# Expert jobs of a routed feed-forward block: the list one slot earlier, one-hots spread over the slots, the row eviction on ScalarE, three slots for most bits of the second search

## The chip, the cores and the metric

The kernel runs on one core of a Trainium2 chip. The metric is the device time of one execution in microseconds, the median of several runs. TensorE (PE, with its weight loads shown as PEld) multiplies matrices and transposes through an identity; VectorE (DVE) and ScalarE (ACT) read its results from PSUM; GpSimd (POOL) issues the indirect transfers that gather and scatter rows by index; SyncE (SP) issues the plain transfers. Each engine takes its own instructions in the order of the program[...].

## The reference

An attention block is followed by a routed feed-forward block. Sixteen sequences of 256 tokens, width 256, pass through layer norms, attention with 16 heads and an output projection, and leave 4096 token rows. What matters here is the second half:

```
tok = x.reshape(-1, d)
gate = jax.nn.softmax(tok @ Wgate.T, axis=-1)
k_cap = bs // E                                   # 4096 // 8 = 512
vals, idx = jax.lax.top_k(gate.T, k_cap)          # each expert takes its 512 best tokens
w = vals.T
g = _ln(tok[idx_flat], mlp_g, mlp_b).reshape(k_cap, E, d)
y = gelu(einsum('ked,ehd->keh', g, fc1s) + b1s)   # 256 -> 1024
y = einsum('keh,edh->ked', y, fc2s) + b2s         # 1024 -> 256
tok = tok.at[idx_flat].add((y * w[..., None]).reshape(-1, d))
```

Each of 8 experts chooses its 512 tokens with the largest gate, normalises those rows, runs a two-layer network on them, scales the result by the gate and adds it back to the token rows.

## The kernel before

The first 930 us are the attention of the 16 sequences, laid out by a table of due times (`plan`). The table also holds the first routing and expert job 0 and most of the list of job 1. After it stands a loop written out by hand, the part that the change touches.

**Two routings.** The 512 tokens of an expert are found in two halves of 256. The first routing (`first`) looks at sequences 0 to 14 only (30 tiles of 128 tokens), so it can be done while the last sequence is still at work. The second (`second`) looks at all 32 tiles, without the tokens already chosen. So there are 16 jobs of 256 rows: jobs 0 to 7 from the first routing, jobs 8 to 15 from the second.

**The search.** A routing finds each expert's threshold bit by bit, 30 bits from 29 to 0. One bit is a round trip: `compare` (L776, DVE) counts the gates that reach the candidate, `count` (L783, PE) adds the counts over the partitions with a tiny bf16 matmul, and `drop` and `step` (L788, L795, DVE) make the next candidate. After the last bit come `masks`, `totals`, `place`, `turn_places` and `split` (L806 to L849), which give every chosen token its place among the 256. `second_routing` is a generator that hands out one list of such steps per slot; it is empty in many slots.

**A job.** `load` (L869 to L873, SP) fetches the weights w1 and w2, 1 MB each, and the bias b2. `gives` (L879, L887, DVE) prepares the values that the list carries, `onehot` (L897, DVE) one 128x128 bf16 one-hot matrix per token tile, `list_matmul` (L906, PE) multiplies the two over 30 or 32 tiles into the list of 256 token numbers and gates, `take` (L914 to L920, DVE) turns it into indices, and `gather` (L925, POOL) fetches the 256 rows in two indirect transfers of 128. `transposes` (L934, PE) turns the rows into `px`, `evict` (L941) scales and shifts them into `xT`. `up` and `gelu` (L953 on PE, L960 on ACT) are the first layer, `down` (L969, PE) the second, `finish` (L975, L976, DVE) adds the bias and multiplies by the gate, `scatter` (L979, POOL) adds the rows to the output, twice per job.

**The slots.** Job k (k = 1 to 15) runs in 16 slots. Slots 0 to 7 each hold one `up` and its `gelu`; slots 8 to 15 each a quarter of a `down`, with `finish` and `scatter` at the ends of slots 11 and 15. Everything else is placed in these slots by hand: the steps of the second routing first, then work for job k+1 (`new`: its remaining one-hots, its list, its transposes) and for job k+2 (`far`: its `gives` and first one-hots). The order of the calls in a slot is the order on each engine, so a DVE step waits behind every DVE step called before it. At the end of job k stands `far.load()`: w1 of job k+2 needs the buffer of w1 of job k and so goes out when the eight `up` are done, w2 after the last `down`. In job 7 (`late`), the next job is the first of the second routing, whose places are only known by then, so all its one-hots are made in job 7 itself.

Of the kernel before, what the change touches and what calls it, by code (L numbers as in the profile page):

```python
# [12 lines left out]
AF = mybir.ActivationFunctionType  # L13
ALU = mybir.AluOpType
# [11 lines left out]
NT = NTOK // P  # L26
# [3 lines left out]
FC = DD // P  # L30
# [7 lines left out]
LN1_G, LN1_B, B_ADA, MLP_G, MLP_B = 0, 2, 4, 6, 8  # L38
# [5 lines left out]
def kernel(  # L44
# [14 lines left out]
    nc = tc.nc  # L59
# [7 lines left out]
    vec = const.tile([P, NVEC], F32, name="vec")  # L67
# [306 lines left out]
    if True:  # L374
# [80 lines left out]
        class First:  # L455
# [22 lines left out]
            def evict(self):  # L478
                b = self.b
                hTs[b] = seq.tile([P, DC, N], F32, tag="hT", name=f"hT{b}")  # L480
                for c in range(DC):
                    nc.scalar.activation(
                        hTs[b][:, c, :], self.pt[:, c, :], AF.Identity,
                        bias=bias1[:, c, b : b + 1],
                        scale=vec[:, LN1_G + c : LN1_G + c + 1],
                    )
# [258 lines left out]
        class Routing:  # L745
# [46 lines left out]
            def step(self, n):  # L792

                old, self.cand = self.cand, bit.tile([P, 1], I32, tag="cand", name="cand")
                nc.vector.scalar_tensor_tensor(  # L795
                    self.cand, self.dropped, (1 << n) >> 1, old,
                    ALU.bitwise_or, ALU.bitwise_xor,
                )
# [62 lines left out]
        class Job:  # L861
# [76 lines left out]
            def evict(self):  # L938
                self.xT = seq.tile([P, DC, CAPL], F32, tag="hT", name="xT")
                for c in range(DC):  # L940
                    nc.vector.tensor_scalar(  # L941
                        self.xT[:, c, :], self.px[:, c, :],
                        vec[:, MLP_G + c : MLP_G + c + 1], vec[:, MLP_B + c : MLP_B + c + 1],
                        ALU.mult, ALU.add,
                    )
                self.hid = seq.tile([P, FC, CAPL], F32, tag="qT", name="hid")
                self.y = work.tile([P, KL, D], F32, tag="pr", bufs=6, name="y")
                self.ph, self.py = {}, {}
# [57 lines left out]
        for b in range(B):  # L1006
# [3 lines left out]
            a = First(b)  # L1010
# [4 lines left out]
            for (g, t), p in its["group"].items():  # L1015
                a = Group(b, g, t)
# [6 lines left out]
            for (d, *ij), p in its["quad"].items():  # L1023
                a = quads[d]
# [6 lines left out]
            for t in range(TB):  # L1031
                a = Tail(b, t)
# [17 lines left out]
        jobs = [Job(e, r, n) for r, n in ((first, n1), (second, NT)) for e in range(E)]  # L1050
# [17 lines left out]

        def second_routing():
            a, b = stretches[2], second
            yield from ([a.shift], [a.exp], [a.divide, a.parts], [], [b.turn], [b.evict])
            new = [partial(b.compare, 29)]
            for n in range(29, -1, -1):
                yield new
                yield []
                new = [partial(f, n) for f in (b.count, b.drop, b.step)]
                new.append(partial(b.compare, n - 1) if n else b.masks)
            yield from (new, [], [b.totals, b.place], [], [], [], [b.turn_places], [b.split])  # L1080

        rest = second_routing()
        last = len(jobs) // 2 - 2
        jobs[2].load()
        jobs[2].gives()
        jobs[2].onehot(0, NT // 2)
        for k in range(1, len(jobs)):
            a = jobs[k]
            new = jobs[k + 1] if k + 1 < len(jobs) else None
            far = jobs[k + 2] if k + 2 < len(jobs) else None  # L1090
            late = k == last + 1
            for s in range(2 * FC):
                for step in next(rest, ()):
                    step()
                if new and s < 4:
                    if late and s == 0:
                        new.gives()
                    h = 0 if late else NT // 2
                    w = (NT - h) // 4
                    new.onehot(h + w * s, h + w * s + w)  # L1100
                if new and s == (7 if late else 6):
                    new.list_matmul(0, NT)
                    new.take()
                    new.gather()
                if new and s == 14:
                    new.transposes()
                    new.evict()
                if far and k != last and s in (9, 10, 12, 13, 15):
                    if s == 9:
                        far.gives()  # L1110
                    else:
                        w = {10: 0, 12: 1, 13: 2, 15: 3}[s]
                        far.onehot(w * NT // 8, (w + 1) * NT // 8)
                if s < FC:
                    a.up(s)
                    a.gelu(s)
                else:
                    i, q = divmod(s - FC, 4)
                    a.down(i, 2 * q, 2 * q + 2)
                    if q == 3:  # L1120
                        a.finish(i)
                        a.scatter(i)
            if far:
                far.load()
# [50 lines left out]
```

## Time and profile before

| | before |
|---|---|
| median of 3 runs | 1227.76 us (1226.0 to 1229.04) |
| the profiled execution | 1229.52 us, its span 1227.8 us |
| PE busy | 1175.4 us (96%) |
| DVE busy | 777.0 us (63%) |
| ACT busy | 602.2 us (49%) |
| POOL busy | 590.7 us (48%) |
| mean granted TensorE clock | 0.989 |

Length of jobs 1 to 14, from the start of the first `up` of one job to that of the next (the timeline of PE gives the starts; the table of windows gives the lengths and the DVE busy time):

| job | 1 | 2 | 3 | 4 | 5 | 6 | 7 | 8 | 9 | 10 | 11 | 12 | 13 | 14 |
|---|---|---|---|---|---|---|---|---|---|---|---|---|---|---|
| us | 20.91 | 17.21 | 17.22 | 17.20 | 17.35 | 16.03 | 17.64 | 16.14 | 15.92 | 16.27 | 16.31 | 15.87 | 16.11 | 15.14 |
| DVE busy | 15.30 | 14.25 | 14.25 | 14.23 | 15.40 | 5.39 | 12.31 | 9.03 | 9.02 | 9.03 | 9.02 | 9.02 | 9.03 | 5.68 |

All times are of one execution and count from the start of its span. A line of the timeline gives the start, the length, the engine, the source line and the operation with its output and inputs, a count of merged instructions, and in brackets how long the engine had been idle and what ended that. A float32 matmul shows as two records, so "x8" of a 128x256 matmul is four matmuls, two slots. In the table of windows each engine's busy time in a stretch stands with its number of instructions, and "PEclk" is the share of the TensorE clock that was granted. Lengths of PE records overlap, since matmuls are pipelined; starts are used for sums.

### The profile page before, as it was taken

The numbers are of one execution on the slowest core, as the hardware profiler recorded it, in microseconds if no ns is written. First come the engines' busy times: TensorE is split into PE (matmuls) and PEld (weight loads), VectorE is DVE, ScalarE is ACT, GpSimd is POOL, SyncE is SP. The second block draws the span as 40 slices with busy tenths as digits, with TensorE's granted clock in tenths as the row PEclk, the third lists the DMA queues.
The fourth block names the chain that finished last, engine by engine and source line by source line (L and its number), as shares of the span: only waits on it lengthen the run. The fifth ranks groups of instructions, "written<-read, shape, count | busy, mean of one in ns | idle before, by whom it ended". The sixth has DMA issues, their size and how long they took to land. (4 is left out here: it accounts for less than half of the span.)

```text
span 1227.8 us, 19464 instructions
## 1 busy us (share of the span) xinstructions
PE 1175.4 (96%) x6784; PEld 812.7 (66%) x6784; DVE 777.0 (63%) x2276; ACT 602.2 (49%) x1669; POOL 590.7 (48%) x818
## 2 busy tenths in 40 slices
PE   6999999999999999999999999999977899999996
PEld 3556666667576666666675766667645777888885
DVE  7556665756665666657566656665677488565551
ACT  2655565555555555655555555557562312222221
POOL 4555555645455555556454555555654223323332
PEclk9999999999999999999999999999988999999998
DMA  5000000000000000000000000000200565555561
GB/s 181 1 1 5 22 6 22 9 18 14 14 15 13 27 5 23 5 22 10 18 15 13 18 10 26 6 14 14 95 1 14 177 179 148 170 174 161 162 178 26
DMA packets 46739, 62.41 MB, mean 51 GB/s; under 512 B 3888, under 2 KB 39984, under 8 KB 46640
## 3 DMA queue, kind: packets, MB, share of 16 engines
q1 hardware_dynamic: 39808, 52.70, 12.9%
q0 software_dynamic: 6144, 8.39, 3.9%
q8 instruction: 54, 0.88, 0.3%
q14 instruction: 45, 0.37, 0.1%
q10 hardware_dynamic: 688, 0.06, 0.0%
HBM read 48.56 MB, written 12.58 MB: 50 GB/s over the span
## 5 line engine op out<-in xcount | busy, mean ns | idle before, releaser
L608 POOL TENSOR_SCALAR pr<-pr,sums 128x256 f32<-128x256 f32 x512 | 238.7, 484 | 276.8 <-DVE sums L604 258.5
L506 PE MATMUL pm<-wq,hT 128*128 128x512 f32 x768 | 357.4, 604 | 5.4 <-DMA wq<-in_wqkvT 3.4
L597 ACT ACTIVATE pr<-sc,nmax 128x256 f32<-128x256 f32 x512 | 236.4, 476 | 162.5 <-DVE nmax L588 148.0
L82 POOL TENSOR_TENSOR ss<-ss,neghalf 128x8 f32<-128x8 f32 x128 | 210.4, 1648 | 99.0 <-DVE ss L527 96.7
L506 PEld LDWEIGHTS pm<-wq,hT 128*128 128x128 f32 x768 | 138.1, 192 | 148.9 <-issue 138.7
L588 DVE TENSOR_REDUCE nmax<-sc 128x2 f32<-128x512 f32 x256 | 164.5, 681 | 45.6 <-PE sc L581 45.5
L960 ACT ACTIVATE hid<-ph,vec 128x256 f32<-128x256 f32 x128 | 60.2, 473 | 209.0 <-PE ph L953 206.2
L523 DVE TENSOR_REDUCE ss<-sq 128x8 f32<-128x512 f32 x128 | 87.4, 683 | 108.8 <-ACT sq L519 108.7
L617 PEld LDWEIGHTS pp<-ident,pr 128*128 128x128 f32 x1024 | 118.5, 143 | 34.9 <-issue 19.6
L617 PE MATMUL pp<-ident,pr 128*128 128x128 f32 x1024 | 137.8, 275 | 3.3 <-ACT pr L597 2.5
L635 PE MATMUL po<-prT,v 128*64 128x256 f32 x1024 | 137.7, 391 | 0.7 <-ACT oT L645 0.7
L581 PE MATMUL sc<-kT,qT 64*128 64x256 f32 x1024 | 131.2, 394 | 0.0
L519 ACT ACTIVATE sq<-pm 128x512 f32<-128x512 f32 x128 | 77.1, 602 | 91.5 <-PE pm L506 90.2
L953 PE MATMUL ph<-xT,w 128*128 128x256 f32 x512 | 121.0, 388 | 0.6 <-DVE xT L941 0.5
L659 PE MATMUL pw<-wo,oT 128*128 128x256 f32 x512 | 119.3, 386 | 0.0
L581 PEld LDWEIGHTS sc<-kT,qT 64*128 64x128 f32 x1024 | 94.7, 188 | 34.8 <-issue 23.6
L969 PE MATMUL py<-w,hid 128*128 128x256 f32 x512 | 117.0, 381 | 0.0
L953 PEld LDWEIGHTS ph<-xT,w 128*128 128x128 f32 x512 | 95.7, 192 | 17.8 <-issue 3.5
L979 POOL DMA_INDIRECT out<-y,idx x32 | 51.1, 1596 | 116.6 <-DVE y L976 35.9
L597 ACT ACTIVATION_READ_ACCUMULATOR pr<-sc,nmax 128x1 f32 x512 | 105.8, 207 | 0.0
L659 PEld LDWEIGHTS pw<-wo,oT 128*128 128x128 f32 x512 | 96.2, 193 | 13.1 <-issue 0.8
L625 DVE COPY prT<-pp 128x512 f32<-128x512 f32 x112 | 76.9, 687 | 43.6 <-PE pp L617 42.7
(118 smaller groups left out, 1295.7 us busy)
## 6 DMA issues: line engine op xcount, KB each, us to landing
w<-in_fc1T SPq DMA_DIRECT2D x16, 1024.0 KB, 5.4
w<-in_fc2T SPq DMA_DIRECT2D x16, 1024.0 KB, 5.4
xs<-in_x SPq DMA_DIRECT2D x16, 256.0 KB, 2.8
out<-tok SPq DMA_DIRECT2D x32, 128.0 KB, 1.7
xn_dram<-tn SPq DMA_DIRECT2D x32, 128.0 KB, 1.7
wq<-in_wqkvT SPq DMA_DIRECT2D x6, 512.0 KB, 8.7
b<-in_b2s SPq DMA_DIRECT2D x16, 128.0 KB, 5.4
wo<-in_woutT SPq DMA_DIRECT2D x1, 1024.0 KB, 10.2
```

The source lines that it names most:

```text
L82: nc.gpsimd.tensor_tensor(dst, src, neghalf[:, : src.shape[1]], ALU.pow)
L506: nc.tensor.matmul(self.pm, hTs[self.b][:, c, bass.ts(self.t, P)], wq[:, c, bass.ts(self.g, GW)], start=(c == 0), stop=(c == DC - 1),)
L523: nc.vector.tensor_reduce(self.ss[:, 0, :], self.sq.rearrange("p (h d) -> p h d", d=HD), AX.X, ALU.add,)
L581: nc.tensor.matmul(self.sc[i, j][:, t, :], qTs[self.b][rows, hp, bass.ts(t, P)], kTs[self.b][rows, hp, :], start=True, stop=True,)
L588: nc.vector.tensor_reduce(self.nmax[i, j], self.sc[i, j], AX.X, ALU.max, negate=True)
L597: nc.scalar.activation(self.pr[i, j][:, t, :], self.sc[i, j][:, t, :], AF.Exp, bias=self.nmax[i, j][:, t : t + 1], scale=1.0, accum_out=se ...
L608: nc.gpsimd.tensor_scalar(self.pr[i, j][:, t, :], self.pr[i, j][:, t, :], self.sums[i][:, 1, j, t : t + 1], 1.0, ALU.mult, ALU.mult,)
L617: nc.tensor.transpose(self.pp[i, j][:, c, bass.ts(t, P)], self.pr[i, j][:, t, bass.ts(c, P)], ident,)
L635: nc.tensor.matmul(self.po[j * HD : (j + 1) * HD, i, :], vs[self.b][:, c, bass.ts(4 * self.d + 2 * i + j, HD)], self.prT[i, j][:, c, :], s ...
L659: nc.tensor.matmul(self.pw, oTs[self.b][:, hp, bass.ts(self.t, P)], wo[:, hp, :], start=(hp == 0), stop=(hp == HP - 1),)
L953: nc.tensor.matmul(self.ph[f], self.w1[:, c, bass.ts(f, P)], self.xT[:, c, :], start=(c == 0), stop=(c == DC - 1),)
L969: nc.tensor.matmul(self.py[i], self.hid[:, f, bass.ts(i, P)], self.w2[:, f, :], start=(f == 0), stop=(f == FC - 1),)
```

## The change

Four things change, all in the expert jobs.

- `Job.evict` (L941): the scale and shift from `px` to `xT` is done by ScalarE (`activation`, Identity, with scale and bias per partition) in two instructions, and no longer by two `tensor_scalar` of VectorE. This holds for all 16 jobs, the two in the table of due times too.
- The list (`list_matmul`, `take`, `gather`) of job k+1 stands in slot 5 of job k, where it stood in slot 6. The transposes stay in slot 14. In job 7 the list stays in slot 7.
- The one-hots: `lay_out` makes the `gives` in slot 6 and then two one-hots in each of slots 7 to 15 and three in each of slots 0 to 4 of the next job. Before, the `gives` stood in slot 9, four one-hots in each of slots 10, 12, 13 and 15, and four in each of slots 0 to 3. In job 7 the next job's one-hots are six in each of slots 0 to 5, where they were eight in each of slots 0 to 3. Before job 1, 18 one-hots of job 2 are made, where 16 were.
- The second search: bits 29 to 11 take three slots each, where they took two; bits 10 to 0 still take two. Two empty slots are added ahead of `turn`. The last step, `split`, falls in slot 14 of job 6; before it fell in slot 9 of job 5.

```diff
             def evict(self):
                 self.xT = seq.tile([P, DC, CAPL], F32, tag="hT", name="xT")
                 for c in range(DC):
-                    nc.vector.tensor_scalar(
-                        self.xT[:, c, :], self.px[:, c, :],
-                        vec[:, MLP_G + c : MLP_G + c + 1], vec[:, MLP_B + c : MLP_B + c + 1],
-                        ALU.mult, ALU.add,
+                    nc.scalar.activation(
+                        self.xT[:, c, :], self.px[:, c, :], AF.Identity,
+                        bias=vec[:, MLP_B + c : MLP_B + c + 1],
+                        scale=vec[:, MLP_G + c : MLP_G + c + 1],
                     )
...
+        LIST_AT, TURN_AT, LATE_AT = 5, 14, 7
+        SLOTS = 2 * FC
+
         def second_routing():
             a, b = stretches[2], second
-            yield from ([a.shift], [a.exp], [a.divide, a.parts], [], [b.turn], [b.evict])
+            yield from ([a.shift], [a.exp], [a.divide, a.parts], [], [], [], [b.turn], [b.evict])
             new = [partial(b.compare, 29)]
             for n in range(29, -1, -1):
-                yield new
-                yield []
+                yield from (new, [])
+                if n > 10:
+                    yield []
                 new = [partial(f, n) for f in (b.count, b.drop, b.step)]
                 new.append(partial(b.compare, n - 1) if n else b.masks)
             yield from (new, [], [b.totals, b.place], [], [], [], [b.turn_places], [b.split])
 
+        def lay_out(job):
+
+            job.gives()
+            for a in list(range(0, 18, 2)) + list(range(18, NT, 3)):
+                yield
+                job.onehot(a, a + (2 if a < 18 else 3))
+
         jobs[2].load()
-        jobs[2].gives()
-        jobs[2].onehot(0, NT // 2)
+        parts = lay_out(jobs[2])
+        for _ in range(10):
+            next(parts)
...
-                if new and s < 4:
-                    if late and s == 0:
-                        new.gives()
-                    h = 0 if late else NT // 2
-                    w = (NT - h) // 4
-                    new.onehot(h + w * s, h + w * s + w)
-                if new and s == (7 if late else 6):
+                if late and s == 0:
+                    new.gives()
+                if late and s < 6:
+                    new.onehot(6 * s, 6 * s + 6)
+                if new and s == (LATE_AT if late else LIST_AT):
+                    for _ in () if late else parts:
+                        pass
                     new.list_matmul(0, NT)
                     new.take()
                     new.gather()
-                if new and s == 14:
+                if new and s == TURN_AT:
                     new.transposes()
                     new.evict()
-                if far and k != last and s in (9, 10, 12, 13, 15):
-                    if s == 9:
-                        far.gives()
-                    else:
-                        w = {10: 0, 12: 1, 13: 2, 15: 3}[s]
-                        far.onehot(w * NT // 8, (w + 1) * NT // 8)
+                if not late and s < LIST_AT:
+                    next(parts, None)
+                if far and k != last and s > LIST_AT:
+                    if s == LIST_AT + 1:
+                        parts = lay_out(far)
+                    next(parts)
```

More of the change, by code (lines that the diff above doesn't have):

```diff
@@ L1091 @@
             late = k == last + 1
-            for s in range(2 * FC):
+            for s in range(SLOTS):
                 for step in next(rest, ()):
                     step()
-                if new and s < 4:
-                    if late and s == 0:
-                        new.gives()
-                    h = 0 if late else NT // 2
-                    w = (NT - h) // 4
-                    new.onehot(h + w * s, h + w * s + w)
-                if new and s == (7 if late else 6):
+                if late and s == 0:
[5 more added lines that the diff above has]
+                        pass
                     new.list_matmul(0, NT)
```

## The prediction

> **What bounds the kernel now.** I read the page's busy times first, then the jobs as windows, then the timeline inside a job of each kind, and last what PE waits for. TensorE is busy 96% of the span, so only PE's gaps and slow stretches can be won, and the change touches the last 270 us alone. The table of windows, one row a job (columns: window, length, then busy time of PE, PEld, DVE, ACT, POOL with counts, granted clock, DMA share, GB/s):
>
> ```profile
> 968.59:989.50 20.91, 17.87 (x107) 14.53 (x105) 15.30 (x81) 6.35 (x11) 8.08 (x10) 0.92 0.54 148
> 989.50:1006.71 17.21, 16.38 (x107) 13.29 (x107) 14.25 (x75) 3.79 (x8) 5.17 (x4) 1.00 0.55 160
> ...
> 1140.48:1156.79 16.31, 15.37 (x102) 13.30 (x101) 9.02 (x45) 3.79 (x8) 5.18 (x4) 1.00 0.60 170
> ...
> 1188.77:1203.91 15.14, 15.14 (x102) 13.35 (x100) 5.68 (x26) 3.79 (x8) 5.18 (x4) 1.00 0.42 108
> ```
>
> Job 14 is what a job costs when PE never waits: 15.14 us. The eight slots of `up` in job 15 take 6.91 us (1203.91 to 1210.82), so a slot is 0.864 us; sixteen are 13.82, the list about 0.8, the transposes about 0.5. Jobs 8 to 13 have 0.7 to 1.2 us more, jobs 2 to 5 some 2.1, job 1 5.8. There are three causes.
>
> *Search (jobs 1 to 5).* PE's timeline of job 3:
>
> ```profile
> 1006.71 2.02 PE L953 MATMUL ph<-xT,w 128*128 128x256 f32 x8 [0.15 <-DVE xT L941]
> 1009.31 0.16 PE L783 MATMUL pc<-cnt,block 128*128 128x1 bf16 x1 [0.59 <-DVE reach L776]
> 1009.34 1.97 PE L953 MATMUL ph<-xT,w 128*128 128x256 f32 x8
> 1011.40 0.18 PE L783 MATMUL pc<-cnt,block 128*128 128x1 bf16 x1
> 1011.44 1.97 PE L953 MATMUL ph<-xT,w 128*128 128x256 f32 x8
> 1013.25 0.17 PE L783 MATMUL pc<-cnt,block 128*128 128x1 bf16 x1
> ```
>
> A pair of slots with its count takes 1.84 us when nothing is late (1011.44 to 1013.25 is 1.81). So a count costs 1.84 − 2 × 0.864 = 0.11. The first pair takes 2.60, the second 2.10: the counts wait for `reach`, 0.76 and 0.26 lost. Why `reach` is late, in DVE's timeline around the same boundary (job 3 begins at 1006.71):
>
> ```profile
> 1006.11 0.99 DVE L941 TENSOR_SCALAR xT<-px,vec 128x256 f32<-128x256 f32 x2
> 1007.02 0.73 DVE L897 TENSOR_SCALAR oh<-lane,partf 128x128 bf16<-128x128 bf16 x4
> 1007.67 0.42 DVE L975 TENSOR_TENSOR y<-py,b 128x256 f32<-128x256 f32 x1
> 1008.12 0.35 DVE L976 TENSOR_SCALAR y<-y,w 128x256 f32<-128x256 f32 x1
> 1008.39 0.15 DVE L788 TENSOR_SCALAR drop<-pc 128x1 int32<-128x1 f32 x1
> 1008.57 0.16 DVE L795 SCALAR_TENSOR_TENSOR cand<-drop,cand 128x1 int32<-128x1 int32 x1
> 1008.77 0.48 DVE L776 TENSOR_SCALAR_CACHE_REDUCE reach<-gT,cand 128x256 bf16<-128x256 f32 x1
> ```
>
> The round trip itself is 0.87 us, but it stands behind `xT`, four one-hots and `finish`. The first `up` waits for `xT` too (0.15). With 8 counts a stall-free job is 15.14 + 0.88 − 0.05 (30 list tiles, not 32) = 15.97; jobs 2, 3 and 4 lose 1.24, 1.25 and 1.23.
>
> *Gather (jobs 6 to 13).* The timeline of job 11, from the list on:
>
> ```profile
> 1145.66 0.95 PE L906 MATMUL pls<-give,oh 128*128 128x10 bf16 x32
> 1146.65 0.17 DVE L914 COPY ls<-pls 128x10 f32<-128x10 f32 x1 [2.54 <-PE pls L906]
> 1147.80 1.01 POOL L925 DMA_INDIRECT xg<-xn_dram,idx  x1 [4.46 <-PE ph L953]
> 1148.47 0.37 SPq L869 DMA_DIRECT2D w<-in_fc1T  x1
> 1149.12 0.98 POOL L925 DMA_INDIRECT xg<-xn_dram,idx  x1 [0.30 <-issue]
> 1154.67 0.55 PE L934 MATMUL px<-ident,xg 128*128 128x128 f32 x3 [0.94 <-DMA xg<-xn_dram,idx]
> ```
>
> The second gather is issued 0.65 us after the 1 MB load of w1 and lands 6.1 after that load's issue; PE is at the transposes 5.0 after it. Over 1151 to 1153 us the DMA view gives the plain queue 200 packets (98.9% of the engines) and the gather queue 7 with no data: the second gather is held until w1 is through.
>
> *Job 1.* PE waits 2.88 us for `gate_of`, which stands behind 24 one-hots on DVE, and then runs at a granted clock of 0.50 (window 976 to 978 us).
>
> **What the Trainium skill says.** "TensorE: Matmul & The Clock Gate", Part 1: an idle window of about 3.4 us halves PE's clock for about as long. The trace agrees: 0.50 after job 1's stall, and 1.00 in every other job, with stalls up to 2.1 us. "ScalarE: Activation LUTs", Table sets: identity sits in every table set, so it brings no reload. The trace agrees for another set: 32 Identity evictions of `hT` (L482) stand between exponentials and squares, and the whole run has five table loads of 1.28 us. "DMA: Bandwidth & Descriptors", Queues, rings and completion order: each DMA engine takes turns between queues, a packet at a time. Here the measurement decides: the gather that came second got nothing for 2 us.
>
> **The change part by part.** DVE's one-hots cost 0.165 us each (16 in 2.64, timeline of job 1), `finish` 0.73 once PE is done, the round trip 0.87, `gives` 0.77, all from DVE's timelines. T is the start of a job.
>
> 1. *Search at three slots a bit, xT off DVE.* In jobs 2 to 4 DVE now does: `finish` from T+0.2 to T+0.93, then three one-hots (0.5) in each of slots 0 to 3, and one round trip in about 2.7 us. The three phases by hand: a count in slot 1, its round trip over by T+2.3, the next count in slot 4 at T+3.6; a count in slot 0, over by T+1.8, next T+2.7; a count in slot 2, over by T+3.05, next T+4.4. None is late. The last one-hot is done by T+3.8 to T+4.7; the list begins at T+4.5 and takes 0.75, so its last tile is there in time. Jobs 2 to 4 lose nothing: gain 3.7. Job 5 stalled 17.35 − (15.09 + 2 × 0.11 + 0.36 for `totals` and `turn_places`) = 1.68; its counts (slots 1, 3, 5, now two slots a bit) find `reach` ready at T+2.4 and T+4.3 against T+2.7 and T+4.5: gain 1.6. The counts themselves and `totals` only change jobs. The cover of 0.2 to 0.3 us there is the thinnest; without it each late bit costs what it is late.
>
> 2. *List a slot earlier.* Gathers go out 0.864 earlier, w1 does not move: the issues stand 1.53 and 0.21 us before w1, where they stood 0.67 before and 0.65 after. In jobs 2 and 4 they stand 1.12 before and 0.19 after, and PE, there at 5.36 after w1's issue (1004.18 − 998.82 in job 2), finds the rows landed; in jobs 8 to 13 they come 5.7 to 6.2 after it. I take 5.3 plus 0.1 for the release: PE needs the second gather at 5.1, so about 0.3 us of waiting stays. Jobs 8 to 13 fall to 15.14 + 0.3: gain 96.62 − 92.64 = 4.0. Bounds: no earlier landing, 0; the second gather ahead of w1, all 5.8. Job 6, which now carries four counts, `totals` and `turn_places` (0.8 us that job 5 and earlier give up), gives PE 0.5 us more between w1 and the transposes, so its 0.9 of wait goes: gain 0.9. In job 14 no w1 moves and nothing waited: 0.
>
> 3. *Job 1.* `gate_of` no longer holds PE in slot 4, but the list now stands in slot 5 and needs 30 one-hots: 18 end at T+4.6, `shift` and 6 more at T+5.9, `divide` at T+6.4, the last 6 at T+7.35. PE is there at T+4.3 and leaves the list at about T+7.55, then does `up` 5, the turn and `up` 6 at T+8.8 (full clock) or T+9.8 (halved). Before, `up` 6 began at 979.60, T+11.0: gain 1.2 to 2.2. What is late next is the gather: POOL does `parts` until T+10.1, so the rows can hold the transposes; I take 1.5. The first `up` of job 2 waits no more for DVE's xT: 0.2.
>
> 4. *Eviction on ScalarE.* DVE: two of 538 ns. ACT: two of 561 by the nearest row (L482, same shape from PSUM), after 8 slots of idling, so hidden; uncovered it would be 0.05. In the table of due times, `xT` of job 0 no longer waits for one-hots, and `tok`, `ls` and the gather of job 1 come 0.9 us earlier, so the transposes of job 1 find rows: the PE idle of 0.52 and part of the 0.16: gain 0.6. Queued behind `xT` of job 1 on ACT are the last two `gelu` of job 0: ready at about 961.8, needed at 962.0.
>
> 5. *Job 7.* The list stays. But `gives` of job 9 (0.77) now stands before `take`: 0.4 later. The rows wait for w1 either way: −0.1 (0 to −0.5).
>
> Sum: 3.7 + 1.6 + 4.0 + 0.9 + 1.5 + 0.2 + 0.6 − 0.1 = 12.4; I take off 0.4 for thin covers: 12.0. The profiled execution would go from 1229.5 (span 1227.8) to 1217.5 (span 1215.8); the median of the runs is 1.8 below that execution: 1227.76 − 12.0 = 1215.8.
>
> **The rivals.**
> *The early list buys nothing:* the rows land with w1's end whatever the issue. For it: 7 packets in 2 us. Against: 5.3 in jobs 2 and 4. Gain 12.0 − 4.0 = 8.0: 1219.8.
> *The second gather slips ahead of w1:* all waits go, +1.8, and job 1 at full clock, +0.4: 1213.5.
> *The stall moves to the list:* if DVE's work takes 10% longer than read, 0.5 in the first 4.7 us of a job, counts and lists in jobs 1 to 6 are late by about that: 12.0 − 3.0 = 9.0, 1218.8. Against: the covers of 0.3 to 0.9.
> *Slower: ScalarE reloads its tables for each xT.* From the transposes to `xT` it is then 0.2 + 1.28 + 1.12 = 2.6 us against the 1.73 of the two slots that PE has to do: 0.9 late in each of jobs 1 to 15, 13.5 in all, 1227.8 − 12.0 + 13.5 = 1229.3; from 0.8 an eviction it takes the whole gain. Against: L482, and the changed program holds as many table loads as the old.
>
> **How the numbers follow.** Forecast 0.60, early list for nothing 0.15, gather ahead 0.15, list late 0.06, reload or another loss 0.04. The low end, 1212, holds the second rival; the high end, 1220.5, the first and third. Worst of the bounds together: 1222. About 0.3% (3.7 us) is what can be told from no change; all but the last case lie beyond it: faster 0.94, same 0.02, slower 0.04.
>
> **What would show it.** Right: jobs 2 to 4 at 15.6 to 15.8 us, job 5 at 16.0, jobs 8 to 13 at 15.4 with a DMA wait of about 0.3 at L934, job 1 near 19.2, no PE wait for `reach`, no table load more. Wrong: jobs 8 to 13 at 16; PE waiting at L906 for `oh`; a clock below 1 in job 7; px waiting longer in job 1 than the stall it lost.

## The result and the profile after

| | before | after |
|---|---|---|
| median of 6 runs each, taken in turn | 1228.12 us (1226.0 to 1231.06) | 1218.84 us (1216.32 to 1221.41) |
| ratio | | 0.9924, 95% interval 0.9903 to 0.9945 |
| the profiled execution | 1229.52 us, span 1227.8 us | 1216.65 us, span 1214.6 us |

The kernel became 9.3 us faster (the interval: 6.8 to 11.9). The profiled execution after is the second fastest of its six, so the two profiles differ by 12.9 us and show more gain than the runs. The jobs alone, 1 to 14, went from 235.32 to 223.59 us.

The table of windows after, one row a job (columns as before: window, length, busy time of PE, PEld, DVE, ACT, POOL, granted clock, DMA share, GB/s), for jobs 1, 3, 7, 11 and 14:

```profile
967.21:985.56 18.35, 17.43 (x103) 14.45 (x102) 14.24 (x77) 7.26 (x13) 8.12 (x10) 1.00 0.56 155
...
1001.24:1017.14 15.90, 15.90 (x106) 13.44 (x105) 11.96 (x61) 4.80 (x10) 5.25 (x4) 1.00 0.63 176
...
1064.36:1080.21 15.85, 15.71 (x101) 13.44 (x100) 11.62 (x63) 4.80 (x10) 5.19 (x4) 1.00 0.60 179
...
1128.11:1144.00 15.89, 15.36 (x101) 13.30 (x100) 8.06 (x42) 4.81 (x10) 5.24 (x4) 1.00 0.62 175
1175.67:1190.81 15.14, 15.14 (x102) 13.35 (x101) 4.25 (x21) 4.80 (x10) 5.18 (x4) 1.00 0.39 107
```

In job 3 PE's busy time is now the whole length. Job 11 still has 0.53 us that PE doesn't fill. Job 7, which was 17.64 us, has nearly none; the forecast didn't have that.

PE's timeline at the start of job 3, to be held against the one shown of before:

```profile
1001.21 0.17 PE L783 MATMUL pc<-cnt,block 128*128 128x1 bf16 x1
1001.24 2.84 PE L953 MATMUL ph<-xT,w 128*128 128x256 f32 x12
1003.91 0.17 PE L783 MATMUL pc<-cnt,block 128*128 128x1 bf16 x1
1003.94 1.97 PE L953 MATMUL ph<-xT,w 128*128 128x256 f32 x8
```

No bracket is left: three slots (12 records) lie between two counts, neither the first `up` nor the next count waits. DVE's timeline at the same place shows why: `reach` is begun 1.28 us after the job's start (2.06 before), ahead of the one-hots.

```profile
1002.52 0.48 DVE L776 TENSOR_SCALAR_CACHE_REDUCE reach<-gT,cand 128x256 bf16<-128x256 f32 x1
...
1002.93 1.69 DVE L897 TENSOR_SCALAR oh<-lane,partf 128x128 bf16<-128x128 bf16 x8
```

The timeline of job 11 from the list on:

```profile
1134.57 1.01 POOL L925 DMA_INDIRECT xg<-xn_dram,idx  x1 [3.51 <-PE ph L953]
1135.88 0.98 POOL L925 DMA_INDIRECT xg<-xn_dram,idx  x1 [0.30 <-issue]
1136.10 0.37 SPq L869 DMA_DIRECT2D w<-in_fc1T  x1
1141.09 0.27 PE L934 MATMUL px<-ident,xg 128*128 128x128 f32 x1
...
1141.89 0.55 PE L934 MATMUL px<-ident,xg 128*128 128x128 f32 x3 [0.53 <-DMA xg<-xn_dram,idx]
```

The second gather now goes out 0.22 us ahead of w1, as forecast, and yet PE stands at the second transposes until 5.79 us after w1's issue. PE's list of waits over jobs 1 to 15 has two rows left (columns: total us, times, longest us); before there were also `gate_of` 2.9, `reach` 2.4, `mask` 0.5 and `xT` 0.5.

```profile
PE px L934 <- DMA xg<-xn_dram,idx: 3.5, 7, 0.7
PE pls L906 <- DVE oh L897: 0.7, 2, 0.5
```

Set against the forecast's steps, with a second pair of profiles (both kernels profiled once more, below):

| jobs | forecast gain, us | first pair | second pair |
|---|---|---|---|
| 2 to 6 (search, and the rows of job 6) | 3.7 + 1.6 + 0.9 = 6.2 | 6.21 | 5.69 |
| 8 to 13 (rows) | 4.0 | 1.16 | 2.91 |
| 1 | 1.5 + 0.2 = 1.7 | 2.56 | 1.25 |
| 7 | −0.1 | 1.78 | 1.69 |
| 14 | 0 | 0 | 0 |
| 1 to 14 | 11.8 | 11.73 | 11.51 |

The sum is right because wrong terms cancel: jobs 8 to 13 gave 0.3 to 0.7 of what was forecast, and job 7 gave 1.7 us that was not forecast at all (job 1 gave 0.9 us too much in the first pair and 0.5 too little in the second). The jobs give 11.5 to 11.7 us and the runs 9.3 (6.8 to 11.9); over the profiles of all kernels in this document, the time outside jobs 1 to 14 is anywhere from 989.7 to 995.7 us, so a total tells less than the jobs do. The experiments are about these two terms, and about which part of the change carries the search term.

### The profile page after: what moved, and what is told of

It reads as the page before. It is cut to its first block, busy times and chain, and to the rows that moved or that the text cites. A ratio compares the mean times of both kernels' runs of the same rounds, so it can differ in the third digit from the quotient of the medians.

```text
span 1214.6 us, 19466 instructions
## 1 busy us (share of the span) xinstructions
PE 1171.7 (96%) x6784; PEld 813.2 (67%) x6784; DVE 764.5 (63%) x2244; ACT 618.2 (51%) x1701; POOL 591.0 (49%) x818
## 5 line engine op out<-in xcount | busy, mean ns | idle before, releaser
L953 PE MATMUL ph<-xT,w 128*128 128x256 f32 x512 | 118.3, 384 | 0.0
L969 PEld LDWEIGHTS py<-w,hid 128*128 128x128 f32 x512 | 94.9, 190 | 13.1
```

Source lines behind the costliest of these rows:

```text
L953: nc.tensor.matmul(self.ph[f], self.w1[:, c, bass.ts(f, P)], self.xT[:, c, :], start=(c == 0), stop=(c == DC - 1),)
L969: nc.tensor.matmul(self.py[i], self.hid[:, f, bass.ts(i, P)], self.w2[:, f, :], start=(f == 0), stop=(f == FC - 1),)
```

## The experiments

Not all kernels ran on the same chip, but each ran beside the kernel before, so kernels from different chips are compared by their ratio to before.

### The same two kernels again

No edit.

> The kernel before, profiled a second time, to see what belongs to a run and not to the change. If the 6.8 and 7.1 us landings of job 7's two gathers (counted from the issue of w1) come from the order of the work, they come again and job 7 takes 17.6 us. If they were stragglers of one execution, job 7 takes about 1.5 us less, near 16. The jobs 8 to 13 should again take 15.9 to 16.3 us; the start of the first up of job 0 may differ by 1 to 3 us, as PE's clock differs in the attention.

> The changed kernel once more, with more rounds against the kernel before. Jobs 2 to 5 at 15.5 to 15.9 us and jobs 8 to 13 at 15.6 to 16.1, as in the first profile; the whole 8 to 13 us under the kernel before, depending on where PE's slow clock windows fall.

Measured: before 1226.8 us once, beside 1229.3 (1226.54 to 1230.33, 15 runs) on that chip; after 1218.38 us (1217.13 to 1219.7), ratio 0.9919, interval 0.99 to 0.9938. Jobs 2 to 6 keep their lengths from one profile to the other within 0.3 us, job 7 is 17.65 before and 15.96 after; jobs 8 to 13 after sum to 93.64, where the first profile had 95.46. So job 7 is systematic, and the rows' wait differs between executions of one kernel. Job 1 after is 19.32, where it was 18.35:

```profile
968.23:987.55 19.32, 18.58 (x103) 15.40 (x102) 14.32 (x77) 7.26 (x13) 8.16 (x10) 0.91 0.53 145
```

The work is the same (103 matmul records), the clock is 0.91 and not 1.00: the difference is PE's speed after the list.

### Where the rows' wait comes from: the list's slot, and w1

Two theories stand in these expectations. W: the load of w1 holds up a gather issued shortly before it or after it, so w1 is what matters. R: the rows land a fixed time after their own issue, so the list's slot is what matters.

The list back in slot 6, all else as changed:

```diff
-        LIST_AT, TURN_AT, LATE_AT = 5, 14, 7
+        LIST_AT, TURN_AT, LATE_AT = 6, 14, 7
```

> The changed kernel with the list back in slot 6, everything else as changed. Theory W (the load of w1 holds the second gather until it is through, so the rows land 5.5 to 6.1 us after w1's issue whenever the gather goes out after 0.5 us before w1): jobs 8 to 13 take the same within 0.3 us, near 16.1, and the time differs from the changed kernel by 0 to 2 us. Theory R (a gather takes its time from its own issue): the rows land 0.86 us later, jobs 8 to 13 take 16.7, 5 us more in all.

Measured: 1223.8 us (1222.14 to 1226.65), ratio 0.9964 (0.9955 to 0.9973), 5.4 us above the changed kernel on the same chip. Against the first profile after, 2.1 us are in jobs 8 to 13 (97.52), 2.2 in jobs 2 to 6, 1.6 in job 1, where an `up` waits 2.6 us for a `gelu` of ScalarE, a wait that the changed kernel doesn't have. Of the 2.2 in jobs 2 to 6 about 1.8 are waits for rows too: the second transposes stand 5.38 to 6.23 us after w1's issue there, where they stood 5.32 to 5.45. So neither theory has the number: the slot is worth 5.4, but only 2.1 of it (3.9 against the second profile) where R places it.

The list in slot 4 (`LIST_AT` 4), on another chip:

> The changed kernel with the list one slot earlier still, in slot 4. Theory W, that the load of w1 holds a gather issued shortly before it: the second gather then goes out 1.08 us before w1, lands about 2.2 us after w1's issue, and jobs 8 to 13 are at 15.14 to 15.2, 1.0 to 2.8 us less in all; but in jobs 1 to 6 PE is at the list some 0.9 us before the last one-hots, 0.3 to 0.9 lost in each, 3 us: in sum 0 to 2 us slower than the changed kernel. Theory R, that the landing only shifts with the issue: jobs 8 to 13 still wait, the rows at 4.5 to 5.0 after w1's issue, 15.2 to 15.5, and the sum is 1 us slower. What tells them apart is where the second transposes stand after w1: 5.0 with no DMA wait, with rows landed by 2.2 (W), or by 4.6 (R).

Measured: 1216.22 us (1213.63 to 1217.04), ratio 0.9897 (0.9874 to 0.992). Jobs 8 to 13 are 15.14 each, with no wait for rows; the second gather goes out 1.08 us ahead of w1, and by the packet records its last row moves 1.46 us after w1's issue. That is nearer to W's 2.2 than to R's 4.6. The cost in jobs 2 to 6, feared at 3 us, isn't there (78.82 against 78.80): with the list a slot earlier PE loses nothing at it there. Job 1 takes 20.25 us, at a mean clock of 0.92.

w1 of job k+2 issued by ScalarE behind the eviction in slot 14, the list left in slot 5:

```diff
                     new.transposes()
                     new.evict()
+                    if far:
+                        far.load_w1(nc.scalar)
...
-                self.w1 = seq.tile([P, DC, DD], F32, tag="v", name="w1")
-                nc.sync.dma_start(self.w1, fc1T[e].rearrange("(c p) f -> p c f", p=P))
+                if self.w1 is None:
+                    self.load_w1(nc.sync)
```

`load_w1` is the two removed lines, with the queue as an argument.

> The changed kernel with the load of w1 issued by ScalarE behind the eviction in slot 14, and no longer by SyncE in slot 8. Theory W: the second gather meets no weight load, lands about 2.8 us after its own issue, as in job 14, PE never waits for rows, jobs 8 to 13 take 15.14 us, and the whole is about 5 us faster than the changed kernel, near 1212 to 1214. Theory R: the landing stays 5.7 us or more after the issue and jobs 8 to 13 stay at 15.6 to 16.1. A loss would show if w1, now overlapping w2 at the start of the next job, held the next gather: rows would then land after slot 14.

Measured: 1214.18 us (1213.34 to 1215.32), ratio 0.9884 (0.9866 to 0.9902); each of its four runs lies below each of the changed kernel's on the same chip. The timeline of job 11 (lines of the kernel are four further down here):

```profile
1135.96 0.98 POOL L929 DMA_INDIRECT xg<-xn_dram,idx  x1 [0.30 <-issue]
...
1140.30 0.60 PE L938 MATMUL px<-ident,xg 128*128 128x128 f32 x4
...
1141.10 0.37 ACTq L868 DMA_DIRECT2D w<-in_fc1T  x1
```

The second gather goes out 8.64 us into the job, where it went out 7.77 us into it in the changed kernel (in jobs 8 to 13 it goes out 7.8 to 8.7 us in, never earlier than before this edit), the four transposes follow one another without a bracket, and w1 goes out behind them. Jobs 8 to 13 are 15.14 each. W holds: with w1 out of the way nobody waits for rows, though the gathers start no earlier.

The same move of w1 in the kernel before:

> The kernel before, in all its parts, with only the load of w1 of job k+2 moved: ScalarE issues it after the eviction in slot 14 of job k (behind VectorE's eviction here), where SyncE issued it after the eighth up. Theory W, the load of w1 is all that the rows waited for, and the list's slot has no worth of its own: jobs 8 to 13 at 15.14, job 6 at 15.4, job 7 at 15.6, jobs 2 to 5 0.1 to 0.3 less each through the rows and otherwise as long as before (16.9 to 17.2); in all 8 to 9 us faster than before (ratio about 0.993), as much as the changed kernel gains in another way. Theory L, the list in slot 6 is too late in itself: the rows, issued at 7.3 and 8.6 us into the job, then land after PE needs them at 13, and jobs 8 to 13 stay at 15.5 or more; 3 to 5 us faster than before.

Measured: 1229.73 us, ratio 1.0003 (0.9991 to 1.0014), jobs 8 to 13 as before (96.82). But it is no test of either theory, since the edit moved nothing in time. The timeline of ScalarE in job 11:

```profile
1148.75 0.47 ACT L964 ACTIVATE hid<-ph,vec 128x256 f32<-128x256 f32 x1 [0.39 <-PE ph L957]
1148.81 0.37 ACTq L868 DMA_DIRECT2D w<-in_fc1T  x1
```

The job began at 1140.75, so w1 went out 8.06 us into it, 0.07 later than before. In the kernel before the eviction is VectorE's: ScalarE has nothing to wait for in slot 14 and issues the load 0.06 us after the start of its last `gelu`. The expectation took a place in the program for a place in time. With the eviction on ScalarE too, the load stands behind a wait for the transposes:

> The kernel before with the eviction on ScalarE, and the load of w1 of job k+2 issued by ScalarE behind that eviction, which waits for the transposes: so the load now really goes out at 13.8 to 14.7 us into job k, where the run with VectorE's eviction left it at 8.06. The list stays in slot 6, the search at two slots a bit. Theory W, w1 is all that the rows waited for: jobs 8 to 13 at 15.14, job 6 at 15.1 to 15.4, job 7 at 15.4 to 15.9, jobs 2 to 5 shorter by 0.03 to 0.3 than with the eviction alone (16.31, 16.64, 16.14, 16.90); 8 us faster than with the eviction alone, ratio about 0.992, as good as the changed kernel. Theory L, a list in slot 6 comes too late in itself: jobs 8 to 13 at 15.5 or more, ratio 0.995 to 0.998.

Measured: 1217.48 us (1215.04 to 1217.84), ratio 0.9905 (0.9887 to 0.9924). PE's waits over jobs 1 to 15:

```profile
PE pgT L757 <- DVE gate_of L727: 2.9, 1, 2.9
PE po L813 <- DVE mask L806: 0.6, 1, 0.6
...
```

No row for `px`: jobs 8 to 13 are 15.14, with the list in slot 6. A list in slot 6 is not too late in itself; it is too late only beside w1. This kernel, with list, one-hots and search as before, is as fast as the changed one.

The packet records put sizes on it. Means over jobs 8 to 13, in us after w1's issue:

| kernel | second gather issued | last packet of w1 | last row of the gathers | second transposes | jobs 8 to 13, sum |
|---|---|---|---|---|---|
| before | 0.65 | 5.29 | 5.60 | 6.00 | 96.62 |
| list in slot 6 | 0.65 | 5.28 | 5.73 | 6.15 | 97.52 |
| after, first profile | −0.22 | 5.27 | 5.28 | 5.81 | 95.46 |
| after, again | −0.22 | 4.98 | 5.08 | 5.51 | 93.64 |
| list in slot 4 | −1.08 | 4.60 | 1.46 | 5.10 | 90.84 |

An issue 0.87 us earlier moved the last row by 0.3 to 0.5: it still comes with w1's end. Another 0.86 earlier moved it by 3.6 to 3.8, ahead of w1. Jobs 2 to 4 of the first profile after lie between: issued 0.33 us ahead of w1 (job 3), the second gather has its last row 4.97 us after w1's issue; issued 0.67 and 0.85 ahead (jobs 4 and 2), at 2.83 and 1.87.

### Which part carries the search term

The eviction back on VectorE, all else as changed:

```diff
-                    nc.scalar.activation(
-                        self.xT[:, c, :], self.px[:, c, :], AF.Identity,
-                        bias=vec[:, MLP_B + c : MLP_B + c + 1],
-                        scale=vec[:, MLP_G + c : MLP_G + c + 1],
-                    )
+                    nc.vector.tensor_scalar(
+                        self.xT[:, c, :], self.px[:, c, :],
+                        vec[:, MLP_G + c : MLP_G + c + 1], vec[:, MLP_B + c : MLP_B + c + 1],
+                        ALU.mult, ALU.add,
+                    )
```

> The changed kernel with the eviction put back on VectorE (two tensor_scalar), all else as changed. Theory A, small share: three slots a bit leave DVE room for 0.99 us at the start of a job, so what returns is the wait of the first up for xT, about 0.2 in jobs 2 to 6, and a late count of 0.1 to 0.3 in jobs 2 to 4: jobs 2 to 4 at 15.9 to 16.2, in all 1.5 us slower than the changed kernel (ratio to the kernel before about 0.993). Theory B, half of the search term is the eviction: jobs 2 to 4 go back by 0.7 to 1.0 each and the list waits for one-hots in jobs 2 to 6, in all 4 us slower (0.995 to 0.996). On job 7: if the eviction is what took its 1.8 us off, it goes back to 17.6; otherwise it stays at 15.9 to 16.0.

Two slots for all bits, all else as changed:

```diff
-                if n > 10:
+                if n > 99:
```

> The changed kernel with two slots for all 30 bits of the second search, the search now ending in job 5 again; all else as changed. Theory A, spacing is half: with xT off DVE and three one-hots a slot, a bit still has 0.87 of round trip plus 0.99 of one-hots in 1.84 us, with finish of 0.73 ahead, so one or two counts of jobs 2 to 5 are late by 0.3 to 0.5 each: jobs 2 to 4 at 16.4 to 16.8 (four more counts than in the changed kernel cost 0.2 to 0.3 of that), job 6 at 15.3 to 15.5; in all 2 us slower than the changed kernel (ratio to before about 0.9935). Theory B, the spacing is the whole search term: jobs 2 to 4 back at 17.2, in all 5 us slower (0.996). Theory C, the spacing is nothing once the eviction is away: within 0.5 us of the changed kernel (0.992). On job 7: if the search was what lengthened it, it goes back to 17.6.

The eviction alone, in the kernel before (the first diff the other way round):

> The kernel before with the eviction alone moved to ScalarE. Theory A: what DVE no longer does at the start of a job, 0.99 us, comes off the first late count: jobs 2 to 5 gain 0.7 to 0.9 each and 0.15 at the first up, jobs 8 to 13 nothing, the table 0.6: in all 4 us faster than before (ratio about 0.9965). Theory B: the next late thing takes its place, 1 us or less (0.999). Theory C, ScalarE is the worse place: from 0.2 us more in each of 15 jobs, 3 us slower (1.0025). On job 7: if the eviction takes its 1.8 us off, it is at 15.9 here; otherwise 17.6.

Measured:

| kernel | median, us | ratio | jobs 2 to 6, sum | job 7 |
|---|---|---|---|---|
| eviction back on VectorE | 1217.39 (1215.33 to 1220.6) | 0.9904 (0.9884 to 0.9925) | 78.92 | 16.15 |
| two slots for all bits | 1219.37 (1218.1 to 1220.04) | 0.9923 (0.9903 to 0.9942) | 79.76 | 17.49 |
| eviction alone | 1225.99 (1222.16 to 1228.89) | 0.9985 (0.9975 to 0.9994) | 81.85 | 17.42 |
| after, two profiles | | | 78.80, 79.24 | 15.86, 15.96 |
| before, two profiles | | | 85.01, 84.93 | 17.64, 17.65 |

In the changed kernel the eviction is worth nothing that can be told: neither theory expected that. With VectorE's eviction and three slots a bit, PE has no wait for `xT` or `reach`. The third slot is worth 0.5 to 1.0 us in jobs 2 to 6. PE's timeline of job 3 with two slots a bit:

```profile
1004.72 0.17 PE L783 MATMUL pc<-cnt,block 128*128 128x1 bf16 x1
1004.75 1.97 PE L953 MATMUL ph<-xT,w 128*128 128x256 f32 x8
1006.58 0.16 PE L783 MATMUL pc<-cnt,block 128*128 128x1 bf16 x1
1006.60 1.97 PE L953 MATMUL ph<-xT,w 128*128 128x256 f32 x8
1008.51 0.18 PE L783 MATMUL pc<-cnt,block 128*128 128x1 bf16 x1
```

A pair of slots with its count takes 1.86 there, the next 1.93 (1.84 when nothing is late): with the eviction away and three one-hots a slot in place of four, two slots are nearly enough. The eviction alone, with the one-hots as they were, takes 3.1 to 3.2 us off jobs 2 to 6, half of the 6; its runs gain 2.0 (0.7 to 3.1). So the term has no single owner: three parts each give DVE room, and in both pairs that were run (eviction with one-hots, one-hots with the third slot) the part left out was worth at most 1.0 us. The third pair was not run, and the list's slot, which goes with the one-hots in both pairs, is worth 2.2 us in these jobs (list back in slot 6), most of it through the rows.

### Job 7

The rows of job 7 don't wait for the list: in both kernels the gathers go out after w1, by 0.19 and 1.51 us before, by 0.55 and 1.87 after. Yet the last row moved 6.63 us after w1's issue before, and 5.11 after. The DMA view of both kernels in 40 equal slices, with the row of the queue that carries instructions. First before, from 1086.7 to 1090 us:

```profile
DMA  9494989799939040100300000300001010099499
...
q8 instruction: 1, 0.02, 1.7%
```

Then after, from 1076.4 to 1080 us:

```profile
DMA  8998999999570100000000000060000009929978
...
q8 instruction: 1, 0.02, 1.6%
```

Before, a trail of single packets follows the block; they are the last rows, and the transposes begin at 1089.73. After, the block ends and nothing follows until the 6, which is the 16 KB packet of the instruction queue, at 1078.80. Before, that packet started at 1087.48, inside the block, 4.6 us after w1's issue, and took 0.88 us.

Two kernels were made to move it: the changed kernel with one count's matmul issued several times into the same tile.

```diff
-                nc.tensor.matmul(self.pc, block, self.cnt, start=True, stop=True)
+                for _ in range(7 if n == 20 and self is second else 1):
+                    nc.tensor.matmul(self.pc, block, self.cnt, start=True, stop=True)
```

> The changed kernel with one of the second search's matmuls (bit 20, job 3 or 4) issued seven times into the same tile instead of once: six tiny matmuls more with their weight loads, 0.1 us each, nothing else. Theory F: job 7 was long before (17.6) because a 16 KB transfer of the instruction queue fell at 12.8 to 13.0 us into the job, among the rows of the gather; in the changed kernel it falls just after the transposes (14.5), because TensorE's instructions stand elsewhere in its stream. Twelve instructions more ahead of job 7 put it back to between 12 and 13 us into the job, and job 7 goes from 15.9 to between 16.8 and 17.6, with a DMA wait of 0.8 to 1.6 at the first transpose. Theory S: job 7 became short because the search no longer ends in job 5 or through DVE's work in job 7; then it stays at 15.9 to 16.1 here, wherever the transfer falls. The extra counts cost 0.4 to 0.7 in the job that has them under either theory; in all 0.5 us (S) or 1.5 to 2.3 us (F) slower than the changed kernel.

> The changed kernel with the matmul of one count (bit 20) issued three times instead of once: two tiny matmuls and two weight loads more, 0.2 us. What is asked is where the 16 KB transfer of the instruction queue falls in job 7, and what job 7 then takes. Theory F (the transfer delays the rows when it falls among them): if it starts 4.0 to 5.0 us after w1's issue, the last row lands 6.4 us or more after that issue and job 7 takes 17.0 to 17.7; if it starts between 1 us before and 4 us after, it delays w1 and job 7 takes 16.3 to 17.0; if it starts after 5.2, job 7 takes 15.8 to 16.2. Theory S (job 7 is short because the search ends in job 6): 15.8 to 16.2 wherever it falls. The total tells little: 0.2 to 2 us slower than the changed kernel.

Seven issues: 1218.82 us, ratio 0.9916 (0.9888 to 0.9945). The packet did not go to where it was expected; it started 8.25 us into job 7, 0.04 ahead of w1's issue. w1's last packet came at 5.20, and job 7 took 16.63. Three issues: 1220.57 us (1215.21 to 1223.07), ratio 0.9929 (0.9905 to 0.9953); the packet stayed behind the transposes, 6.26 us after w1's issue, and job 7 took 16.06, which both theories allow. All kernels with w1 at its old place, by where the packet starts after w1's issue in job 7:

| packet starts | kernels | last row, us after w1's issue | job 7, us |
|---|---|---|---|
| 4.4 to 4.6 | before (two profiles), eviction alone, two slots, before with w1 on ScalarE's queue | 6.45 to 6.65 | 17.42 to 17.65 |
| −0.04 | seven issues | 5.83 | 16.63 |
| 6.2 or later | after (two profiles), eviction on VectorE, lists in slots 4 and 6, three issues | 5.11 to 5.34 | 15.86 to 16.15 |

Twelve profiles fall in three groups without an overlap, and the kernel that moved the packet left the short group. But the groups are those of the search too: all five kernels of the first row give every bit two slots, and all the others have three for most bits. What tells the theories apart is the order of the packets. The two gathers of job 7 are 64 packets of 4 KB, with small packets of 4 bytes behind them. In each of the five profiles of the first row, 60 of the 64 are through by 5.30 us after w1's issue, and exactly four start later: the first when the 16 KB packet ends (to within 0.02 us), the others one after another behind it. In the before profile the 16 KB packet ends at 1088.36, and the DMA view from 1088.33 to 1089.60 us has these four and two small ones, nothing else:

```profile
DMA  8000000000000800000000000003000030000000
...
q0 software_dynamic: 6, 0.02, 6.0%
```

Four is a sixteenth of 64, and a core has 16 DMA engines. So it looks as if the packet held up the share of the one engine that carried it; the records don't name a packet's engine, so this last step is an inference.

Job 12 agrees. In eight profiles with w1 at its old place a packet of the instruction queue starts there 4.6 to 4.9 us after w1. In four of them a packet of the gather starts just as it ends, and the job takes 16.92 to 17.14 us (seven issues, three issues, list in slot 6) and 16.34 (before with w1 on ScalarE's queue, whose jobs 8 to 13 are 16.1 in the mean). In the other four (after twice, two slots, eviction on VectorE) no packet of the gathers comes at its end or later, and the job takes 15.43 to 15.89. So a transfer among the rows costs time when part of the gather is left behind it, and need not.

So theory F is the better supported. Two things stay open. The packet was never moved on purpose into the 4.4 to 4.6, and what decides its place in job 7 was not found: the search in job 6 goes with the later place. And with seven and three issues the transposes of job 12 begin 1.1 us after the gather's last packet, where the means of jobs 8 to 13 in the table above are 0.4 to 0.5.

## Why the prediction was right

The median is 3.0 us above the 1215.8 of the forecast and inside its range of 1212.0 to 1220.5. The mechanisms of the search and of the rows were right, but that the terms add up so well is in part luck: jobs 8 to 13 gave 2.8 and 1.1 us less than forecast in the two pairs of profiles, and job 7 gave 1.9 and 1.8 more, for a reason that the prediction didn't have. By the prediction's steps:

1. *Search at three slots a bit, xT off DVE.* Right, within 0.1 us a job in the first profile. Jobs 2 to 4 were to be 15.6 to 15.8 and are 15.68, 15.90 and 15.51; job 5 was to be 16.0 and is 15.90; PE has no wait for `reach`. What the step didn't say is that its causes overlap: it read as if the third slot were needed, and two slots do with 0.5 to 1.0 us more.

2. *List a slot earlier.* This is the term that was mis-sized: 4.0 forecast in jobs 8 to 13, 1.16 and 2.91 in the two profiles of the kernel. The failing piece is "I take 5.3 plus 0.1 for the release". The 5.3 came from jobs 2 and 4, where PE finds the rows landed when it gets there, 5.36 after w1's issue; but w1 is through earlier in those two jobs (its last packet at 4.69 and 4.62) than in jobs 8 to 13 (5.29 in the mean before, 5.27 and 4.98 after). For the packet of the last row 5.3 was still fair (5.28 and 5.08); but from that packet to the transposes there are 0.53 and 0.43 us, not 0.1, and before there were 0.40. So the second transposes come at 5.81 and 5.51, not 5.4, and 0.77 and 0.47 us a job stay where 0.3 was to stay. The mechanism was stated rightly (the gather is held until w1 is through). The rival in which the second gather slips ahead of w1 named the escape, but not the lead that it takes: in these jobs 0.22 us was not enough and 1.08, one slot more, was. Job 6 is right: 15.9 forecast, 15.81 measured, with no wait for rows.

3. *Job 1.* 1.7 forecast, 2.56 and 1.25 measured. The list went as worked out (PE left it 7.53 us into the job, 7.55 forecast), and `up` 6 began at 8.71 in the first profile and at 9.79 in the second, where the forecast had 8.8 with full clock and 9.8 with half. "I take 1.5" held a wait for the gather in it; that wait is 0.17 in the first profile and nothing in the second. What makes 18.35 or 19.32 is the clock, 1.00 or 0.91. On the clock, one reading of the prediction was off: it has full clock "with stalls up to 2.1 us", but the longest single stall of PE in jobs 2 to 14 before is the 1.69 us of job 7; 2.1 is what jobs 2 to 5 have over job 14 in all. And the stall of 2.88 us that was followed by half clock, like one of 2.58 with the list in slot 6, is shorter than the idle window of about 3.4 us that the prediction took.

4. *Eviction on ScalarE.* Hidden, as forecast: the two instructions take 1.02 us where 1.12 was taken, and no reload follows. Its 0.6 in the table can't be told: over the profiles of all kernels the first `up` of job 0 starts anywhere from 949.5 to 954.8 us.

5. *Job 7.* Wrong: −0.1 forecast, 1.78 and 1.69 measured. "The rows wait for w1 either way" was true and not the whole: before, the last of them also waited 1.5 us for something else, by the order of the packets the instruction transfer. The profile before had it in plain sight: job 7 has a wait of 1.69 us at its first transpose, the longest of the eight, and the forecast never asked why that job's rows land 7.1 us after w1 and those of the others 6.

Of the rivals, "the stall moves to the list" stands at 1218.8, the median itself, and yet it is not what happened: PE waits for one-hots in job 1 alone, 0.7 us. Nor did the early list buy nothing (1219.8): put back to slot 6 it costs 5.4 us. A total that agrees says little of its cause. In jobs 8 to 13 the second gather did not slip ahead of w1, and ScalarE reloads nothing (five table loads, as before).

## What to carry to other kernels

When a small transfer that PE waits for goes out near a large one that nobody needs soon, move the large one behind the small one's consumer; here that alone, with the eviction that makes it possible, gave as much as the whole change, and added to it made the fastest kernel (1214.18 us). A DMA issue is late only if its engine has something to wait for there: look up the issue's time, not its place in the program. A wait that is longer in one of many equal jobs wants its own cause before it is counted with the others.

## What the runs showed of the hardware

A gather of 128 rows issued 0.22 us ahead of a 1 MB load on another queue was as good as held until that load was through; issued 0.67 and 0.85 ahead (jobs 4 and 2) its last row came 2.83 and 1.87 us after the load's issue, issued 1.08 ahead (list in slot 4) 1.46 us after it. The Trainium skill, "DMA: Bandwidth & Descriptors", Queues, rings and completion order, has the engines take turns between queues; in these runs the measurement differs, as it did in the profile before.

The load of w1 itself took 4.98 to 5.29 us with gathers beside it (means of jobs 8 to 13) and 4.60 with the gathers gone ahead.

Instructions come by DMA too: in the jobs of the kernel after, a 16 KB packet of the instruction queue starts every 16 to 24 us and takes 0.9 to 1.0 us, and in job 7 such a packet among the rows went with a last row 1.1 to 1.5 us later. Four of the gathers' 64 packets started only when it ended; the other 60 were through before.

In job 1 the 30 tiles of the list drip in over 3.2 us, with gaps of 0.27 and 0.47 us between groups of tiny matmuls:

```profile
972.40 0.99 PE L906 MATMUL pls<-give,oh 128*128 128x10 bf16 x6 [0.27 <-DVE oh L897]
973.87 1.02 PE L906 MATMUL pls<-give,oh 128*128 128x10 bf16 x6 [0.47 <-DVE oh L897]
```

The mean clock of job 1 was 1.00 in three kernels (after, eviction on VectorE, w1 late) and 0.84 to 0.92 in five profiles with the same drip (after again, two slots, list in slot 4, three and seven issues). So a stretch in which PE works, but thinly, went with a lower clock in five of eight profiles: from 6.6 to 7.0 us into the job, near the end of that stretch, half clock for 3.41 us in four of them and for 6.83 us with three issues. A stall of 2.88 us (job 1 before) or of 2.58 (list in slot 6) was followed by 3.41 us at half clock too, one of 1.69 us (job 7 before) was not.
